# An audio tower on one core: means of the weights taken off by VectorE, a new order in the first group, and the last experts fetched in quarters and halves

## The chip, the core and the metric

The kernel runs on one core of a Trainium2 chip. The metric is the device time of the whole kernel in microseconds. Before the change it is 1425.66 us, the median of three runs (1423.68 to 1425.87). A core has five engines that run side by side: TensorE (in the profile PE for its products and PEld for its weight loads), VectorE (DVE), ScalarE (ACT), GpSimd (POOL) and SyncE (SP), which here only issues transfers. Products land in PSUM, from where VectorE or ScalarE take them to SBUF. The kernel's own schedule decides the order of the instructions of each engine; each engine works its list off in that order and waits for others by semaphores.

## What is computed

```python
h = DCT of frames of 512 samples          # 64 sequences x 157 frames x 512
n = layernorm(h)
key, query = tanh(n @ Wk + bk) * pi, tanh(n @ Wq + bq) * pi     # 4 sets x 8 planes
V = n @ Wv + bv
# per set and plane: cumulative sums of exp(i key) * V over the frames, read with exp(-i query),
# summed with softmax(set_weights); the same with fixed position phases
gate = sigmoid(n @ Wg + bg)
total = gate * total + (1 - gate) * pos_contrib
h = h + n + (total / norm) @ Wo + bo
x = layernorm(h)
# one expert of 16 per sequence, chosen by softmax(mean(x) @ Wg2 + bg2):
h = h + score * (x @ We[chosen] + be[chosen])
```

All is float32. The 64 sequences are handled in 16 groups of four. The DCT is folded into Wv, Wk, Wq and Wg, so that these weights act on the frames directly; the layernorm's mean is taken off by lowering each transformed weight by the part that the mean would carry.

## The kernel before

A group's 640 frames (four sequences of 160 slots) lie in `xT` as four chunks of 128 rows, in two halves of 320 columns. Tiles of 128 columns are numbered 0 to 3 and TAIL. PSUM is used as four buffers (`psum()`) of two banks each, handed out in turn; a new one waits for the readers of the one that had its place.

```python
def fold_once(g, m, engine=nc.gpsimd):           # first folding of the frames for the DCT
    ft = half(S[g]["xT"], m)
    add(even, ft[:, :2], ft[:, 2:])              # VectorE
    engine.tensor_tensor(ft[:, :2], ft[:, :2], ft[:, 2:], ALU.subtract)

def fold_twice(g, m):
    add(ft[:, 2], even[:, 0], even[:, 1])
    sub(ft[:, 3], even[:, 0], even[:, 1])
    for n in range(2):                           # a rotation in two lifting steps
        nc.vector.scalar_tensor_tensor(to, by, lift[:, n:n+1], to, ALU.mult, ALU.add)

def through_dct(raw, k, to, start=True, stop=True):      # a fourth of a weight through the DCT
    for i, (table, r) in enumerate(PARTS[k]):            # six products for the four fourths
        nc.tensor.matmul(to, tables[:, table], raw[:, r], ...)

def add_up(raw, n, tag, engine=nc.vector):       # sum of a weight's four fourths, in two adds

def less_mean(total, k, to):                     # the mean's share, on top of the same PSUM bank
    nc.tensor.matmul(to, tables[:, 6 + k], total, start=False, stop=True)

def centre(raw, total):                          # Wg instead: mean off ahead of the tables
    nc.tensor.matmul(ps, mean, total, start=True, stop=True)
    sub(raw, raw, ps.unsqueeze(1).to_broadcast([P, C, D]))

def embed(g, n): ...               # DCT of a tile: 8 small products into one PSUM buffer
def embed_statistics(g, n): ...    # ScalarE copy, VectorE sums and bn_stats, GpSimd rstd
def embed_res(g, n): ...           # ScalarE: residual from PSUM, which frees the buffer
def value(g, n): ...               # tile @ wv, by_tokens: four products over chunks 0..3
def keep_value(g, n): ...          # VectorE: PSUM * rstd + bv
def spread(g, n): ...              # TensorE: rstd to all rows (a transpose)
def scale(g, n): ...               # VectorE: xT tile * rstd, for keys, queries and gate
def project(g): ...                # keys and queries, ScalarE tanh to u
def phasors(g): ...                # ScalarE: eight sines of u into kf and qf
def gate_part(g, o): ...           # 128 gate columns, ScalarE tanh with bias to gT
def read(g, c): ...                # attention's reading, VectorE times and plus into gT
def weight_sums(w, t): ...         # four VectorE subtractions of 128x512, for later groups
```

The first group:

```python
warm(12)
made = [psum(), psum()]
of = [ps[:, b, :] for ps in made for b in range(2)]
for k in range(2):
    through_dct(raw_v, k, of[k], stop=False)
total = add_up(raw_v, D, "x2T")
for k in range(2, C):
    through_dct(raw_v, k, of[k], stop=False)
total_kq = add_up(raw_kq, 2 * F, "sum2")
fold_once(0, 0, nc.vector)
fold_twice(0, 0)
for k in range(C):
    less_mean(total, k, of[k])
    if k % 2:
        nc.scalar.copy(wv[:, k - 1 : k + 1], made[k // 2])
embed(0, 0)
embed(0, 1)
for k in range(C):
    through_dct(raw_kq, k, ps[:, k], stop=False)
    less_mean(total_kq, k, ps[:, k])
...
value(0, 0)
fold_once(0, 1, nc.vector); fold_twice(0, 1)
value(0, 1)
embed(0, 2); embed(0, 3)
keep(0)                              # keep_value, spread and scale of a tile together
...                                  # values 2, 3, TAIL in the same manner; Wg's sum on GpSimd
next(consts); value(0, TAIL)
fold_once(1, 0)
centre(raw_g, total)
keep(3); keep(TAIL)
...                                  # Wg through the tables, four fourths
project(0)
fold_twice(1, 0)
fold_phases(0)
...                                  # position products and constants
fold_once(1, 1)
for n in range(2):
    embed(1, n); embed_statistics(1, n)
phasors(0)
for n in range(2):
    embed_res(1, n)
# then the gate: per part of it an embedding of group 1, a spread and scale, and two of
# eight weight sums (four for wo, then four for wv); then the reads and the output products
```

The end, behind the last group (g = 15), with the experts of group 14 still to do:

```python
def fetch(g, rooms=(), parts=1, between=lambda: None):
    for k in range(parts):
        rows = ...                               # VectorE: row numbers of the chosen experts
        if k: between()
        for b in range(GB):                      # one indirect transfer per sequence
            nc.gpsimd.indirect_dma_start(out=ws[b][:, n*k : n*(k+1)], in_=of, in_offset=rows[b])

def picks(c):
    if c == 1:
        route_spread(g); pick(g)
        fetch(g, [*flat, all_v...], 2, biases)   # halves; the bias in between

expert(g - 1, ORDER[1], routes)
expert(g - 1, ORDER[2], picks)                   # picks(c) is called ahead of chunk c
...                                              # two more experts of group 14
for c in range(2):                               # chunks 0 and 1 of all five tiles,
    for n, ps in zip(order, banks):
        expert_chunk(g, n, c, ps)                # four products each, one per sequence
for n, ps in zip(order, banks):                  # then 2 and 3, tile by tile
    for c in range(2, C):
        expert_chunk(g, n, c, ps)
    expert_out(g, n, ps)
```

Of the kernel before, what the change touches and what calls it, by code (L numbers as in the profile page):

```python
# [22 lines left out]
P = 128  # L23
C = D // P
H = D // 2
GB = 4
# [20 lines left out]

ORDER = [TAIL, *range(TAIL)]


@with_exitstack
def audio_tower(ctx: ExitStack, tc: tile.TileContext, a, out):
# [30 lines left out]
    def load(name, shape, src=None):  # L83
        t = const.tile(shape, F32, name=name, tag=name)
        nc.sync.dma_start(out=t, in_=a[name] if src is None else src)
        return t
# [5 lines left out]
    def bank():  # L92
        return psum()[:, 0, :]
# [27 lines left out]

    def fold_twice(g, m):

        if g < NG:
            ft, even = half(S[g]["xT"], m), S[g].pop(("even", m))
            add(ft[:, 2], even[:, 0], even[:, 1])
            sub(ft[:, 3], even[:, 0], even[:, 1])
            for n in range(2):
                to, by = ft[:, n], ft[:, 1 - n]
                nc.vector.scalar_tensor_tensor(to, by, lift[:, n : n + 1], to, ALU.mult, ALU.add)  # L130


    def load_raw(name, n, parts=(slice(None),)):
        t = p1.tile([P, C, n], F32, tag="we", name=name, bufs=GB)
        for of in parts:
            nc.sync.dma_start(out=t[:, of], in_=a[name][:, of])
        return t

    tables = p1.tile([P, 6 + C, P], F32, tag="we", name="tables", bufs=GB)
    nc.sync.dma_start(out=tables[:, :6], in_=a["tables"])  # L140
    raw_v = load_raw("wv", D, (slice(1, C, 2), slice(0, C, 2)))
    load_half(0, 0)
    dct_e = load("dct_e", [P, 2, P])
    trig_o = load("trig_o", [P, 2, P + 1])
    lift = load("lift", [P, 2])
    nc.sync.dma_start(out=tables[:, 6:], in_=a["table_sums"].partition_broadcast(P))
    raw_kq = load_raw("wkq", 2 * F)
# [18 lines left out]
    revexp = load("revexp", [P, GB, E])  # L166
    rowbase = load("rowbase", [P, 3])

# [20 lines left out]

    def through_dct(raw, k, to, start=True, stop=True):  # L190

        for i, (table, r) in enumerate(PARTS[k]):
            nc.tensor.matmul(
                to, tables[:, table], raw[:, r], start=start and i == 0, stop=stop and i == len(PARTS[k]) - 1
            )

# [6 lines left out]

    def less_mean(total, k, to):

        nc.tensor.matmul(to, tables[:, 6 + k], total, start=False, stop=True)

    def centre(raw, total):
        ps = bank()
        nc.tensor.matmul(ps, mean, total, start=True, stop=True)
        sub(raw, raw, ps.unsqueeze(1).to_broadcast([P, C, D]))

# [13 lines left out]

    def by_tokens(ps, x, n, w):  # L230

        for c in range(C):
            nc.tensor.matmul(ps, tile_of(x[:, c], n), w[:, c, :], start=(c == 0), stop=(c == C - 1))  # L233
        return ps
# [165 lines left out]
    def value(g, n):  # L400
        s = S[g]
        s["vps", n] = by_tokens(psum()[:, 0, :], s["xT"], n, wv)

# [123 lines left out]

    def phasors(g):
        u = S[g].pop("u")
        for n, to in ((0, kf), (1, qf)):  # L530
            for k in range(2):
                rows = slice(2 * F * k + F * n, 2 * F * k + F * (n + 1))
                to_k = to.rearrange("p s b t -> p (s b t)")[:, HN * k : HN * (k + 1)]
                nc.scalar.activation(to_k[F : 2 * F], u[rows, 0], AF.Sin, scale=PI)
                nc.scalar.activation(to_k[:F], u[rows, 1], AF.Sin, bias=quarter[rows], scale=-PI)
# [181 lines left out]

    def fetch(g, rooms=(), parts=1, between=lambda: None):
        s = S[g]
        ws = [  # L720
            rooms[b] if b < len(rooms) else p1.tile([P, C * D], F32, tag="we", name="we", bufs=GB) for b in range(GB)
        ]
        n = C * D // parts
        of = a["we"].rearrange("r (k n) -> (r k) n", k=parts)
        for k in range(parts):
            rows = t("rows", [P, GB], I32)
            base = rowbase[:, parts + k - 1 : parts + k]
            nc.vector.tensor_scalar(rows, s["rev"], float(-P * parts), base, ALU.mult, ALU.add)
            if k:
                between()  # L730
            for b in range(GB):
                nc.gpsimd.indirect_dma_start(  # L732
                    out=ws[b][:, n * k : n * (k + 1)],
                    out_offset=None,
                    in_=of,
                    in_offset=bass.IndirectOffsetOnAxis(ap=rows[:, b : b + 1], axis=0),
                )
        s["ws"] = [w.rearrange("p (c o) -> p c o", c=C) for w in ws]
# [71 lines left out]
    def first_values():  # L810

        consts = constants()

        def keep(n):
            keep_value(0, n)
            spread(0, n)
            scale(0, n)

        warm(12)
        made = [psum(), psum()]  # L820
        of = [ps[:, b, :] for ps in made for b in range(2)]
        for k in range(2):
            through_dct(raw_v, k, of[k], stop=False)
        total = add_up(raw_v, D, "x2T")
        for k in range(2, C):
            through_dct(raw_v, k, of[k], stop=False)
        total_kq = add_up(raw_kq, 2 * F, "sum2")
        fold_once(0, 0, nc.vector)
        fold_twice(0, 0)
        for k in range(C):  # L830
            less_mean(total, k, of[k])
            if k % 2:
                nc.scalar.copy(wv[:, k - 1 : k + 1], made[k // 2])
        embed(0, 0)
        embed(0, 1)
        ps = bank()[:, : C * 2 * F].rearrange("p (c n) -> p c n", c=C)
        for k in range(C):
            through_dct(raw_kq, k, ps[:, k], stop=False)
            less_mean(total_kq, k, ps[:, k])
        embed_statistics(0, 0)  # L840
        nc.scalar.copy(wkq, ps)
        embed_statistics(0, 1)
        embed_res(0, 0)
        embed_res(0, 1)
        value(0, 0)
        fold_once(0, 1, nc.vector)
        fold_twice(0, 1)
        value(0, 1)
        embed(0, 2)
        embed(0, 3)  # L850
        keep(0)
        embed_statistics(0, 2)
        embed_statistics(0, 3)
        embed_res(0, 2)
        embed_res(0, 3)
        value(0, 2)
        keep(1)
        total = add_up(raw_g, D, "x2T", nc.gpsimd)
        embed(0, TAIL)
        embed_statistics(0, TAIL)  # L860
        embed_res(0, TAIL)
        value(0, 3)
        keep(2)
        next(consts)
        value(0, TAIL)
        fold_once(1, 0)
        centre(raw_g, total)
        keep(3)
        keep(TAIL)
        for k in range(C):  # L870
            if k % 2 == 0:
                ps = psum()
            through_dct(raw_g, k, ps[:, k % 2])
            if k % 2:
                nc.scalar.copy(wg[:, k - 1 : k + 1], ps)
        project(0)
        fold_twice(1, 0)
        fold_phases(0)
        next(consts)
        next(consts)  # L880
        next(consts)
        fold_once(1, 1)
        for n in range(2):
            embed(1, n)
            embed_statistics(1, n)
        phasors(0)
        for n in range(2):
            embed_res(1, n)
        weigh()

    def first_gate():

        made = chain(weight_sums(wo, t_o), weight_sums(wv, t_v))
        for n in range(C):
            gate_part(0, n)
            if n == 0:
                fold_twice(1, 1)
            m = n + 2
            if m < NM:
                embed(1, m)  # L900
                embed_statistics(1, m)
            if n == 1:
                scores(0)
            spread(1, n)
            scale(1, n)
            if m < NM:
                embed_res(1, m)
            add_bo(0, n)
            next(made)
            next(made)  # L910
        spread(1, TAIL)
        scale(1, TAIL)
        add_bo(0, TAIL)
        load_half(2, 0)
        load_half(2, 1)
# [167 lines left out]
    def picks(c):  # L1083
        if c == 1:
            route_spread(g)
            pick(g)
            fetch(g, [*flat, all_v.rearrange("p i c o -> p (i c o)")], 2, biases)

# [23 lines left out]
def _constants():  # L1112
# [15 lines left out]
    def trig(half, n, turn):  # L1128
# [12 lines left out]

    sums = [x.sum(axis=0) for x in tables]
    table_sums = np.concatenate([sums[0] + sums[1], sums[2] + sums[3], sums[4], sums[5]]) / -D
    return {
# [9 lines left out]
        "revexp": f(np.tile(E - np.arange(E), (P, GB, 1))),  # L1154
        "rowbase": f(np.stack([n * (np.arange(P) + P * E) + k for n, k in ((1, 0), (2, 0), (2, 1))], axis=1)),
    }
# [57 lines left out]
```

## Time and profile before

| | before |
|---|---|
| time | 1425.66 us (1423.68 to 1425.87) |
| span of the profiled run | 1421.9 us |
| TensorE busy | 1405.3 us, 99% |
| VectorE busy | 997.3 us, 70% |
| GpSimd busy | 607.1 us, 43% |
| ScalarE busy | 402.0 us, 28% |

Line numbers such as L233 are those of the kernel before, and a line can be that of a helper used in many places: L233 is the product of `by_tokens`, L362 that of the later groups' `product`, L601 that of `read`, L778 that of `expert_chunk`. A product in float32 shows as two passes, so `x8` in a list of TensorE's work are four calls. In brackets stands the time for which the engine was idle before, and what ended it. In a table by stretches of time the columns are the stretch, its length, the busy time and instructions of PE, PEld, DVE, ACT and POOL, the granted TensorE clock (1.00 is full), the transfers' share and GB/s.

### The profile page before, as it was taken

What the parts mean: (1) busy time and instruction counts of PE and PEld (TensorE: products, weight loads), DVE (VectorE), ACT (ScalarE), POOL (GpSimd) and SP (SyncE); (2) the same over time, 40 slices, a digit from 0 to 9 for tenths busy, and PEclk for the clock granted to TensorE, in tenths of its full rate; (3) what the DMA queues carried; (4) which work ended last, traced back from release to release, by engine and by line L of the source; (5) the groups of instructions that cost most, each with busy time, mean ns of one, the idle gap of its engine ahead of it and who ended that gap; (6) DMA issues with size and microseconds to landing.
All of it is one profiled execution on the core that took longest, in us unless ns stands there. A gap on an engine that the chain in (4) does not pass through costs nothing.

```text
span 1421.9 us, 26962 instructions
## 1 busy us (share of the span) xinstructions
PE 1405.3 (99%) x10646; PEld 929.2 (65%) x10646; DVE 997.3 (70%) x2090; ACT 402.0 (28%) x690; POOL 607.1 (43%) x849
## 2 busy tenths in 40 slices
PE   9899999999999999999999999999999999999998
PEld 5477576675757667575675757657586675766762
DVE  5677776777767676677777767677676777767573
ACT  2414242141422314232142422314223142421410
POOL 2354533535444255533535445255442545345322
PEclk9999999999999999999999999999999999999999
DMA  6013204032140322204132040322303232030305
GB/s 219 1 39 125 75 1 177 24 126 75 39 148 16 130 71 109 88 5 167 34 126 75 10 176 16 127 75 76 118 9 134 68 126 74 1 143 22 126 8 192
DMA packets 47485, 119.74 MB, mean 84 GB/s; under 512 B 9264, under 2 KB 26176, under 8 KB 39424
## 3 DMA queue, kind: packets, MB, share of 16 engines
q0 software_dynamic: 11072, 71.31, 13.0%
q1 hardware_dynamic: 35788, 46.06, 11.0%
q8 instruction: 85, 1.39, 0.4%
q10 hardware_dynamic: 500, 0.64, 0.2%
q14 instruction: 40, 0.33, 0.1%
HBM read 97.41 MB, written 20.58 MB: 83 GB/s over the span
## 4 chain that ended last, share of the span: by engine, by line
PE 91%; DVE 3%; POOL 3%; DMA 1%; issue 1%; ACT 0%; SPq 0%; DVEq 0%; POOLq 0%
PE mm L362 26%; PE mm L567 16%; PE mm L778 16%; PE mm L601 9%; PE mm L233 8%; PE mm L674 3%; PE mm L514 2%; PE mm L248 2%; PE mm L250 2%; PE mm L684 1%; POOL rstd L225 1%; PE mm L586 1%; PE mm L548 1%; PE mm L288 1%; DVE st L220 1%
## 5 line engine op out<-in xcount | busy, mean ns | idle before, releaser
L224 POOL TENSOR_SCALAR rstd<-mv 128x1 f32<-128x1 f32 x160 | 53.5, 334 | 536.1 <-DVE mv L222 529.7
L778 PE MATMUL mm<-we,x2T 128*32 128x512 f32 x2400 | 273.2, 595 | 0.5 <-DVE res_t L789 0.5
L778 PEld LDWEIGHTS mm<-we,x2T 128*32 128x32 f32 x2400 | 70.4, 109 | 149.1 <-issue 141.9
L97 DVE TENSOR_TENSOR gT<-mm,gT 128x128 f32<-128x128 f32 (+1 forms) x135 | 87.0, 672 | 88.5 <-PE mm L567 87.0
L609 DVE TENSOR_TENSOR gT<-mm,gT 128x320 f32<-128x320 f32 x256 | 116.9, 487 | 19.1 <-PE mm L601 14.7
L601 PE MATMUL mm<-att,v 32*128 32x192 f32 (+2 forms) x2048 | 127.8, 371 | 0.9 <-ACT res_t L277 0.5
L601 PEld LDWEIGHTS mm<-att,v 32*128 32x128 f32 x2048 | 105.5, 185 | 11.7 <-PE mm L601 2.9
L732 POOL DMA_INDIRECT we<-in_we,rows x60 | 64.3, 1072 | 105.1 <-issue 98.1
L97 DVE TENSOR_TENSOR v<-mm,v 128x512 f32<-128x512 f32 x105 | 70.9, 687 | 52.5 <-PE mm L362 52.5
L577 ACT ACTIVATE gT<-gT,hbg 128x320 f32<-128x320 f32 x120 | 59.6, 554 | 169.0 <-DVE gT L97 169.0
L225 POOL TENSOR_TENSOR rstd<-rstd,power 128x1 f32<-128x1 f32 x160 | 98.6, 616 | 13.4
L97 DVE TENSOR_TENSOR res<-mm,res 128x512 f32<-128x512 f32 x96 | 64.3, 684 | 56.5 <-POOL res L616 41.8
L277 ACT ACTIVATE res<-mm,shift,rstd 128x512 f32<-128x512 f32 x64 | 49.8, 778 | 158.7 <-POOL rstd L263 110.6
L661 ACT ACTIVATE x<-res,shift,rstd 128x512 f32<-128x512 f32 x64 | 52.1, 814 | 139.0 <-DVE res L97 121.9
L362 PE MATMUL mm<-t_o,sum 128*128 128x256 f32 x384 | 88.1, 379 | 0.0
L362 PE MATMUL mm<-t_v,sum 128*128 128x256 f32 x360 | 86.7, 384 | 0.0
L282 POOL TENSOR_TENSOR res<-res,bo 128x512 f32<-128x512 f32 x64 | 86.3, 1377 | 0.2 <-issue 0.2
L789 DVE SCALAR_TENSOR_TENSOR res<-mm,gate,res 128x512 f32<-128x512 f32 x64 | 48.0, 750 | 50.4 <-PE mm L288 36.4
L362 PEld LDWEIGHTS mm<-t_o,sum 128*128 128x128 f32 x384 | 71.9, 190 | 11.0
L616 POOL TENSOR_TENSOR res<-res,u 128x512 f32<-128x512 f32 x48 | 59.6, 1270 | 44.9 <-DVE u L97 44.9
L233 PE MATMUL mm<-wv,xT 128*128 128x512 f32 x160 | 72.0, 594 | 1.1 <-DVE xT L294 0.8
L119 POOL TENSOR_TENSOR xT<-xT 128x640 f32<-128x640 f32 x30 | 46.5, 1550 | 59.7 <-DVE even L97 40.7
(194 smaller groups left out, 2787.8 us busy)
## 6 DMA issues: line engine op xcount, KB each, us to landing
xT<-in_frames SPq DMA_DIRECT2D x32, 640.0 KB, 4.5
out<-res SPq DMA_DIRECT2D x248, 64.0 KB, 1.7
out<-res_t SPq DMA_DIRECT2D x62, 32.0 KB, 1.6
out<-res_t SPq DMA_DIRECT2D x62, 26.0 KB
wv<-in_wv SPq DMA_DIRECT2D x2, 512.0 KB, 5.7
wg<-in_wg SPq DMA_DIRECT2D x1, 1024.0 KB
wo<-in_wo SPq DMA_DIRECT2D x1, 1024.0 KB
we<-in_we,rows POOLq DMA_INDIRECT x60, 8.1
```

The costliest lines, as they stand in the source:

```text
L97: add = lambda *x: nc.vector.tensor_tensor(*x, ALU.add)
L225: nc.gpsimd.tensor_tensor(rstd, rstd, power, ALU.pow)
L233: nc.tensor.matmul(ps, tile_of(x[:, c], n), w[:, c, :], start=(c == 0), stop=(c == C - 1))
L282: nc.gpsimd.tensor_tensor(r, r, bo, ALU.add)
L362: nc.tensor.matmul(ps[:, b, :], lhs[:, c, P * b : P * (b + 1)], w[:, c, :], start=(c == 0), stop=(c == 1))
L567: nc.tensor.matmul(ps[:, o, :HN], w[:, c, o * P : (o + 1) * P], rhs[:, c], start=(c == 0), stop=(c == 1))
L577: nc.scalar.activation(to, to, AF.Tanh, bias=hbg[:, c : c + 1], scale=0.5)
L601: nc.tensor.matmul(to, s["v", n][q, c * P : (c + 1) * P], by, start=(n == 0), stop=(n == TAIL))
L609: nc.vector.tensor_tensor(th, r[:, :, n], th, op)
L616: more = lambda to, x: nc.gpsimd.tensor_tensor(to, to, x, ALU.add)
L732: nc.gpsimd.indirect_dma_start(out=ws[b][:, n * k : n * (k + 1)], out_offset=None, in_=of, in_offset=bass.IndirectOffsetOnAxis(ap=rows[:, ...
L778: nc.tensor.matmul(ps[Q * i : Q * (i + 1), :], s["x2T"][:, c, i, Q * n : Q * (n + 1)], s["ws"][i][:, c, :], start=(c == 0), stop=(c == C - 1),
```

## The change

It has three aims: to have TensorE do less for the weights' means, to order the first group so that TensorE waits less for the other engines, and to let the last expert products begin when a quarter of each expert's matrix is there.

The means: `through_dct` makes each fourth alone; one product with the table of means gives the mean of Wv, ScalarE copies it to SBUF, and VectorE forms `wmean * table_sums[k] + PSUM` straight into `wv`. Wk and Wq are centred ahead of their tables, as Wg is. The table of sums shrinks from 128 columns a fourth to one.

```diff
-        nc.tensor.matmul(to, tables[:, 6 + k], total, start=False, stop=True)
+        nc.tensor.matmul(ps, mean, total, start=True, stop=True)
...
-        warm(12)
-        made = [psum(), psum()]
+        warm(11)
+        side, made = psum(), [psum(), psum()][::-1]
...
+        def less_mean(k):
+            nc.vector.scalar_tensor_tensor(wv[:, k], wmean, table_sums[:, k : k + 1], of[k], ALU.mult, ALU.add)
         for k in range(2):
-            through_dct(raw_v, k, of[k], stop=False)
+            through_dct(raw_v, k, of[k])
         total = add_up(raw_v, D, "x2T")
-        for k in range(2, C):
-            through_dct(raw_v, k, of[k], stop=False)
-        total_kq = add_up(raw_kq, 2 * F, "sum2")
+        through_dct(raw_v, 2, of[2])
+        means(total, side[:, 0, :])
+        nc.scalar.copy(wmean, side[:, 0, :])
+        through_dct(raw_v, 3, of[3])
         fold_once(0, 0, nc.vector)
-        fold_twice(0, 0)
-        for k in range(C):
-            less_mean(total, k, of[k])
-            if k % 2:
-                nc.scalar.copy(wv[:, k - 1 : k + 1], made[k // 2])
+        fold_sums(0, 0)
+        total = add_up(raw_kq, 2 * F, "sum2")
+        means(total, mean_kq)
+        less_mean(2)
+        centre(raw_kq, mean_kq, 2 * F)
+        less_mean(3)
+        rotate(0, 0)
+        for k in range(C):
+            through_dct(raw_kq, k, new_kq[:, k])
+        nc.scalar.copy(wkq, new_kq)
         embed(0, 0)
         embed(0, 1)
+        less_mean(0)
+        less_mean(1)
+        value(0, 0)                      # by_tokens takes the chunks in the order 2, 3, 0, 1
+        fold_once(0, 1)                  # second half on GpSimd, not VectorE
```

The first loads are four transfers (tables 0 to 3, odd fourths of Wv, tables 4 and 5, even fourths) in place of three. The rest of the first group, as the changed kernel has it:

```python
embed_statistics(0, 0); embed_statistics(0, 1); embed_res(0, 0); embed_res(0, 1)
fold_twice(0, 1)
value(0, 1); embed(0, 2); embed(0, 3)
keep_value(0, 0); keep_value(0, 1)
...                                              # statistics and residuals of tiles 2 and 3
value(0, 2)
next(consts)
deviations(0)                                    # spread and scale
total = add_up(raw_g, D, "x2T", nc.gpsimd)
embed(0, TAIL); keep_value(0, 2); ...
value(0, 3)
means(total, ps); deviations(1); centre(raw_g, ps, D)
keep_value(0, 3); value(0, TAIL); deviations(2); keep_value(0, TAIL)
for k in range(2): through_dct(raw_g, k, made[0][:, k])
nc.scalar.copy(wg[:, :2], made[0])
deviations(3); deviations(TAIL)
for k in range(2): through_dct(raw_g, 2 + k, made[1][:, k])
fold_once(1, 0); next(sums); next(sums)          # weight sums of wv are made here
fold_twice(1, 0)
project(0)
nc.scalar.copy(wg[:, 2:], made[1])
fold_phases(0); next(consts); phasors(0, (0,))   # the keys' four sines
next(consts); next(consts)
embed(1, 0); embed_statistics(1, 0)
phasors(0, (1,))                                 # the queries' four
embed_res(1, 0); weigh(); fold_once(1, 1)
next(sums); next(sums)
# first_gate:
gate_part(0, 0); fold_twice(1, 1); embedded(1); deviations(0)   # embedded: embed, statistics, res
gate_part(0, 1); scores(0); embedded(2); deviations(1); weights()   # two weight sums of wo
gate_part(0, 2); embedded(3); embedded(TAIL); deviations(2)
gate_part(0, 3); deviations(3); deviations(TAIL); weights()
# (add_bo of a tile stands behind each deviations, as before)
```

The end:

```diff
+PIECES = [(1, 0), (4, 0), (4, 1), (2, 1)]
...
-        for k in range(parts):
-            rows = t("rows", [P, GB], I32)
+        for parts, k in pieces:          # all row numbers first
+            rows = p2.tile([P, GB], I32, tag="rows", name="rows", bufs=3)
...
-            if k:
+            if i == 1:
                 between()
...
     def picks(c):
-        if c == 1:
+        if c == 0:
...
-            fetch(g, [*flat, all_v.rearrange("p i c o -> p (i c o)")], 2, biases)
+            fetch(g, [*flat, all_v.rearrange("p i c o -> p (i c o)")], PIECES[1:], biases)
```

So the four sequences' first quarters come first, then the bias, the second quarters, and the second halves.

## The prediction

> **What bounds the kernel now.** I read the busy table first: PE 1405.3 us of a 1421.9 us span. TensorE is nearly never idle, so the change can only take TensorE work away or close TensorE's gaps. The chain of waits in order of time shows where it can do so.
>
> ```profile
> 87.60 6.11 PE mm L601 x92
> 93.71 1.92 PE mm L362 x8
> ...
> 181.50 3.43 PE mm L233 x8
> 184.93 10.36 PE mm L362 x48
> ...
> 267.33 3.43 PE mm L233 x8
> 270.77 10.36 PE mm L362 x48
> ```
>
> Columns: start, length, what. The reader is to see the period: 267.33 - 181.50 = 85.83 us a group, TensorE without a gap. The diff leaves the helpers of groups 1 to 14 as they were, so only the time up to 93.71 us (first output product of group 0) and the end behind the last group can move. The timeline of TensorE in group 0:
>
> ```profile
> 12.33 3.60 PE L209 MATMUL mm<-total,tables 128*128 128x512 f32 x8
> 20.00 7.09 PE L233 MATMUL mm<-wv,xT 128*128 128x512 f32 x16
> 29.75 3.70 PE L233 MATMUL mm<-wv,xT 128*128 128x512 f32 x8 [0.78 <-DVE xT L294]
> 45.62 0.30 PE L288 MATMUL mm<-ident,rstd 128*128 128x128 f32 x1 [2.36 <-DVE wg L96]
> 46.19 5.42 PE L196 MATMUL mm<-wg,tables 128*128 128x512 f32 x12 [0.28 <-DVE v L411]
> 63.85 0.84 PE L248 MATMUL mm<-dct_e,xT 128*128 128x128 f32 x4 [2.63 <-issue]
> 84.34 2.09 PE L601 MATMUL mm<-att,v 32*128 32x320 f32 x26 [0.52 <-ACT res_t L277]
> ```
>
> L209 is the mean taken off by eight passes. The brackets are idle time and its cause. Behind the gap at 63.85 stands a PSUM buffer: that embedding wants one which `embed_res(1, 0)` on ScalarE frees, and this is queued behind eight sines. By stretch of time the gap costs twice, as the clock (the third number from the right) shows:
>
> ```profile
> 62.00:63.00 1.00, 0.00 (x0) 0.00 (x0) 0.20 (x1) 0.96 (x3) 0.81 (x3) 1.00 0.00 0
> 66.00:67.00 1.00, 1.00 (x4) 0.72 (x3) 0.00 (x0) 0.99 (x2) 0.00 (x0) 0.50 0.00 0
> ```
>
> At the end, the timeline of GpSimd and of the weight loads, then the two pieces of the chain:
>
> ```profile
> 1388.57 1.07 POOL L732 DMA_INDIRECT wv<-in_we,rows  x1 [8.73 <-DVE logit L744]
> 1392.44 0.94 POOL L732 DMA_INDIRECT t_v<-in_we,rows  x1 [0.30 <-issue]
> 1398.68 0.94 POOL L732 DMA_INDIRECT t_v<-in_we,rows  x1 [0.30 <-issue]
> 1400.28 0.11 PEld L778 LDWEIGHTS mm<-t_v,x2T_last 128*32 128x32 f32 x1 [1.35 <-DMA t_v<-in_we,rows]
> ```
>
> ```profile
> 1392.44 7.80 DMA t_v<-in_we,rows
> 1400.28 17.37 PE mm L778 x154
> ```
>
> TensorE could have begun the last expert products at 1395.56 (its first matmul on `wv`). The fourth half matrix lands at 1400.28: 4.7 us lost. After it come 40 passes at 0.43 us without a gap.
>
> [...] after a gap of 2.63 us, 0.50 was granted near 65.4 to 68.5. [...] the trace has 0.74 for such a SCALAR_TENSOR_TENSOR (L411), which I use. [...] 4.8 us at least, 7.9 median, from issue to landing of 512 KB in this stretch.
>
> **Part 1, Wv's and Wk/Wq's means.** Gone from TensorE: eight passes of L209 on Wv (3.43 us on the chain) and eight small ones on Wk/Wq. Added: one product with the mean table on each (0.87 us as L213, about 0.2). Added on VectorE: four SCALAR_TENSOR_TENSOR of 128x512 from PSUM, 4 x 0.74 = 3.0 us, and a subtraction of 128x256, some 0.4. The weights load in four transfers with 128 KB less ahead of the first product: at about 310 GB/s, 0.4 us earlier, so it starts near 6.6.
>
> VectorE is now the chain here. `wv` is whole at 8.84 as before; add_up 1.23 + 0.69 to 10.76; first folds 2 x 0.82 to 12.45; sums 2 x 0.48 to 13.4; Wk/Wq sum 0.5 to 13.9; then less_mean 0.74, centre 0.4, less_mean 0.74, rotate 1.13, less_mean 2 x 0.74, to 18.4. The first value product needs the last of these and starts at 18.4 against 20.0. So 3.2 us of TensorE work saved gives 1.6 us.
>
> **Part 2, order in the rest of the values.** spread and scale come later, so the token products no longer wait for VectorE's 0.69 (L294) between them. With 6.9 us for values 0 and 1, 1.8 for two embeddings and 3.45 a value, the third starts at 27.1 (29.75 before), the fourth at 31.8 (35.04). The fifth waits for the buffer of the last embedding, near 37.3. Wg's mean product follows GpSimd's add_up, near 35.6, and VectorE takes it off by 39.9 (2.29 us, L96). Now TensorE has the fifth value under that (37.3 to 40.75), where it stood idle for 2.36 us. Wg's table products run 41.0 to 46.6 with two transposes between, and the projection starts at 46.6 against 51.53: 4.9 us.
>
> **Part 3, into the gates.** Projection 2.3 us to 48.9; then ScalarE's tanh (0.53) and the second copy of Wg (1.01), which also frees the PSUM buffer for the position products, to 50.6; these 1.1 and one embedding 0.9; the first gate part starts at 52.6 (56.74). Only one embedding of group 1 precedes it, and `embed_res` stands after the second set of sines, near 57.8, when the gate part (4.3 us, to 56.95) has just ended. The second gate part starts at 58.2 instead of 66.06: 7.9 us, since the 2.63 us gap and the half clock (about 3.1 us x 0.5 = 1.6) both go. Then a new wait: the next embedding needs `embed_res(1, 1)`, behind VectorE's fold_twice(1, 1), sums and statistics, near 64.9, while TensorE is through the scores at 63.65: 1.25 us. The third gate part starts at 66.1 (73.83), the fourth at 72.5 (79.14), the reads at 77.8 (84.34).
>
> The reads then follow VectorE: the last deviations and t_o sums hold it to 79.9, and four reads at 1.93 us each (L609) let TensorE finish the fourth near 85.5 to 86.5. Before, the four t_v subtractions (0.69, 0.71, 0.90 and 1.76 us) stood before the last scaling and held the reads back to 93.64. By hand the first output product comes 7.1 to 8.1 us earlier.
>
> **Part 4, the last experts.** The spread moves one chunk earlier (0.86 us), but VectorE is in order: it takes `logit` at 1386.27, straight after add_bias, in both kernels. So the first fetch stays at 1388.57. Issues are 1.245 us apart (1388.57 + 3 steps of which the first is 1.38) whatever the size: a 1 MB fetch also shows 0.94 us. Quarters double the issues of the first half, from 9 to 13 in all. With 3.8 to 4.5 us from issue to landing for 256 KB (4.8 for 512 KB less 0.6 of data at 420 GB/s, or some queueing): the fourth quarter is issued at 1392.4 and lands near 1396.6; chunk 0 of five tiles takes 4.3 us, to 1400.9; the eighth quarter is issued at 1398.7 and lands at 1402.7: 1.8 us lost; chunk 1 to 1407.0; the fourth half is issued at 1403.7 and lands near 1408.4: 1.4 us lost. The remaining 8.6 us end at 1417.0 against 1417.65. The 3.7 us won at the start are given back twice: about 0.5 us are left, between -1 and +1.5.
>
> **Sum.** 7.6 us in group 0 and 0.5 at the end, 8.1 by hand. A hand schedule leaves out small waits, and VectorE is slower beside GpSimd's work (the same t_v subtraction takes 0.69 to 1.76 us, L96), so I take off 0.8: 7.3 us. 1425.66 - 7.3 is 1418.4.
>
> **Rivals.** (1) VectorE's longer chain at the start eats the saving: between 12.6 and 15.1 TensorE is idle for about 2 us in two pieces, and if the clock falls as it did at 65 us, 3 us of value products run at half speed, another 1.6 us. Against it: the gaps are shorter than 2.63 us. Then about 1420. (2) TensorE's gap in group 0 merely moves from 63 to about 64 us, into the wait for `embed_res(1, 1)`; if GpSimd's fold is slow it grows to 3 us and brings the half clock back: 3 us of the gain gone, about 1421. (3) The quarters overlap better than I think and the end gains 3 us: about 1415. (4) The issue time of thirteen fetches makes the end longer by 1 us: about 1420. The first two would have to come together to leave no gain at all, as nothing in groups 1 to 14 changes.
>
> **Range and chances.** The four spread the time from 1415 to 1422; with a noise of some 1 us (1423.68 to 1425.87 before) the range is 1414.8 to 1421.8. Two per cent is 28.5 us, more than all of TensorE's gaps together (1421.9 - 1405.3 = 16.6) plus the work removed, so faster by over 2% gets 0.01, slower 0.01, the rest 0.98.
>
> **What would show it.** Right: the first value product near 18.4 us, the projection near 46.6, no gap over 2 us between the first and second gate part, the first output product (L362's line) near 86, a group still 85.8 us; at the end two waits for the fourth tile in place of one. Wrong: a granted clock of 0.5 before 30 us, a gap over 2.5 us near 64, or reads that end later than 88; and for the end, a last expert product that ends before 1408 or after 1411 on the new scale (7 us earlier).

## The result, and the profile after

| | before | changed | ratio, 95% interval |
|---|---|---|---|
| time, first series | 1425.76 us | 1430.1 us (1429.49 to 1433.14) | 1.0037 [1.002, 1.0055] |
| time, second series | 1424.93 us | 1428.94 us (1427.87 to 1432.35) | 1.0029 [1.0018, 1.0039] |
| span of the profiled run | 1421.9 us | 1431.4 us | |
| TensorE busy | 1405.3 us | 1409.2 us | |

The kernel became 4 us slower; the prediction was 1418.4 us, 7.3 us faster. Line numbers are those of the changed kernel from here on: L240 is the product of `by_tokens`, L369 that of `product`, L610 that of `read`, L792 that of `expert_chunk`, L295 the transpose of `spread`, L557 the gate part. The chain of waits of the changed kernel, in order of time (start, length, what):

```profile
97.65 1.92 PE mm L369 x8
...
1403.84 0.82 issue
1404.65 0.60 PE mm L792
...
1410.30 16.53 PE mm L792 x146
```

The first line answers to 93.71 of before: the first output product of group 0 comes 3.9 us later, not 7 to 8 earlier. The middle is as predicted: from that product to the first fetch of the last experts it is 1294.8 us (97.65 to 1392.43) against 1294.9 (93.71 to 1388.57). At the end, the last pieces in which TensorE runs through are about the same length (16.53 and 17.37), but what stands ahead of them is new: single passes of 0.6 us with pieces called "issue" between, for which the profile finds no releaser. TensorE's timeline in group 0:

```profile
20.17 7.34 PE L240 MATMUL mm<-wv,xT 128*128 128x512 f32 x16
62.81 0.32 PE L295 MATMUL mm<-ident,rstd 128*128 128x128 f32 x1 [2.18 <-POOL rstd L232]
64.17 6.26 PE L557 MATMUL mm<-xT,wg 128*128 128x320 f32 x16 [1.03 <-ACT res L284]
85.41 0.32 PE L295 MATMUL mm<-ident,rstd 128*128 128x128 f32 x1 [2.14 <-POOL rstd L232]
86.77 3.58 PE L610 MATMUL mm<-att,v 32*128 32x320 f32 x32 [1.04 <-ACT res_t L284]
```

The old gap of 2.63 us at 63.85 is gone, and two gaps of more than 3 us in two pieces each stand in its place, one ahead of the second gate part and one ahead of the reads. By stretch of time, a granted clock of 0.50 follows both (third number from the right):

```profile
66.00:67.00 1.00, 1.00 (x3) 0.68 (x2) 0.95 (x3) 0.38 (x2) 0.00 (x0) 0.50 0.00 0
88.00:89.00 1.00, 1.00 (x16) 0.84 (x12) 1.00 (x1) 0.00 (x0) 1.00 (x2) 0.50 0.65 233
```

So the second gate part takes 6.26 us (5.77 in the kernel before, 4.47 at the granted 1.00 of the first part), and the reads begin slowly. At the end, GpSimd's timeline (first and fourth quarter, then the last half):

```profile
1392.43 1.09 POOL L746 DMA_INDIRECT wv<-in_we,rows  x1 [9.34 <-DVE logit L758]
1396.33 0.95 POOL L746 DMA_INDIRECT t_v<-in_we,rows  x1 [0.30 <-issue]
1407.61 0.94 POOL L746 DMA_INDIRECT t_v<-in_we,rows  x1 [0.30 <-issue]
```

Thirteen issues at 1.25 us, as predicted. But TensorE comes to full speed (four passes at once every 0.43 us) only at 1411.04, 18.6 us after the first issue; before, it was 11.7 (1388.57 to 1400.28).

### The profile page after: what moved, and what is told of

It is laid out like the page before. It is cut to its first block, busy times and chain, and to the rows that moved or that the text cites. A ratio compares the mean times of both kernels' runs of the same rounds, so it can differ in the third digit from the quotient of the medians.

```text
span 1431.4 us, 26950 instructions
## 1 busy us (share of the span) xinstructions
PE 1409.2 (98%) x10632; PEld 929.8 (65%) x10632; DVE 999.8 (70%) x2095; ACT 400.3 (28%) x689; POOL 612.1 (43%) x854
## 4 chain that ended last, share of the span: by engine, by line
PE 90%; DVE 4%; POOL 4%; issue 1%; ACT 1%; DMA 0%; SPq 0%; POOLq 0%; DVEq 0%; ACTq 0%
PE mm L369 26%; PE mm L792 17%; PE mm L576 16%; PE mm L610 9%; PE mm L240 8%; PE mm L683 3%; PE mm L521 2%; PE mm L255 2%; PE mm L257 2%; POOL rstd L232 1%; PE mm L693 1%; DVE st L227 1%; PE mm L595 1%; POOL rstd L231 1%; PE mm L295 1%
## 5 line engine op out<-in xcount | busy, mean ns | idle before, releaser
L792 PE MATMUL mm<-we,x2T 128*32 128x512 f32 x2400 | 273.8, 595 | 0.6 <-DVE res_t L803 0.5
L792 PEld LDWEIGHTS mm<-we,x2T 128*32 128x32 f32 x2400 | 70.5, 109 | 150.1 <-issue 144.1
L610 PE MATMUL mm<-att,v 32*128 32x192 f32 (+2 forms) x2048 | 129.6, 377 | 1.0 <-ACT res_t L284 1.0
L610 PEld LDWEIGHTS mm<-att,v 32*128 32x128 f32 x2048 | 106.6, 188 | 12.3 <-PE mm L610 2.9
L369 PE MATMUL mm<-t_o,sum 128*128 128x256 f32 x384 | 88.1, 379 | 0.0
L369 PE MATMUL mm<-t_v,sum 128*128 128x256 f32 x360 | 86.7, 384 | 0.0
L369 PEld LDWEIGHTS mm<-t_o,sum 128*128 128x128 f32 x384 | 71.9, 190 | 11.0
L240 PE MATMUL mm<-wv,xT 128*128 128x512 f32 x160 | 72.3, 596 | 1.4 <-ACT res_t L284 1.1
```

The source lines that it names most:

```text
L369: nc.tensor.matmul(ps[:, b, :], lhs[:, c, P * b : P * (b + 1)], w[:, c, :], start=(c == 0), stop=(c == 1))
L610: nc.tensor.matmul(to, s["v", n][q, c * P : (c + 1) * P], by, start=(n == 0), stop=(n == TAIL))
L792: nc.tensor.matmul(ps[Q * i : Q * (i + 1), :], s["x2T"][:, c, i, Q * n : Q * (n + 1)], s["ws"][i][:, c, :], start=(c == 0), stop=(c == C - 1),
```

## Experiments

All times against runs of the kernel before on the same chip:

| run | what | us | ratio [95%] |
|---|---|---|---|
| after_again | the changed kernel | 1428.94 | 1.0029 [1.0018, 1.0039] |
| tail_only | before + the new fetch | 1430.73 | 1.0043 [1.0029, 1.0056] |
| group_only | the new first group, old fetch | 1425.38 | 1.0000 [0.9992, 1.0009] |
| loads_back | group_only + old first loads | 1425.44 | 1.0003 [0.9994, 1.0012] |
| idle_issues | before + 4 idle issues behind the weights | 1430.34 | 1.0042 [1.0026, 1.0057] |
| half_quarters | tail_only, half first, quarters last | 1430.32 | 1.0039 [1.0025, 1.0052] |
| late_issues | before + 4 idle issues some 6 us later | 1425.30 | 0.9997 [0.9988, 1.0005] |
| whole | before, 1 MB pieces, 5 issues | 1429.68 | 1.0032 [1.002, 1.0044] |
| order_only | group_only, one order in the gate | 1422.82 | 0.9984 [0.9976, 0.9993] |
| room_only | group_only, two subtractions later | 1423.43 | 0.9986 [0.9978, 0.9995] |
| order_room | both | 1419.41 | 0.9965 [0.9952, 0.9979] |
| order_room_gate | both + a gate part earlier | 1420.50 | 0.9969 [0.9957, 0.998] |

### Which half of the change loses

My first theory was that the first group loses, as its first output product comes 3.9 us later in the profile; the rival was the fetch of the last experts. The edits: tail_only takes `fetch`, `PIECES` and `c == 0` of the change into the kernel before. The other two go the other way:

```
# group_only: the changed kernel with
PIECES = [(1, 0), (2, 0), (2, 1)]        # was (1,0), (4,0), (4,1), (2,1)
if c == 1:                               # was c == 0
# loads_back: group_only with
nc.sync.dma_start(out=tables, in_=a["tables"])       # one transfer, then wv's two
```

> The changed kernel a second time, for a second profile and a firmer time. If its profile is typical, group 0 again ends near 97.6 us (3.9 us later than before) and TensorE crawls again at about 0.7 us a pass between the first quarter's landing and the last half's, with some 36 to 39 us from the first fetch to the end (33.3 before). If the crawl was an accident of that one execution, the stretch from the first fetch to the end is 33 to 35 us. Time 1429.5 to 1431.

> The kernel before with nothing but the new fetches: quarters, quarters, halves, asked for one chunk earlier. Theory G (the loss of 4.3 us lies in the first group, the tail is neutral): within 0.7 us of before. Theory T (thirteen issues and the smaller transfers make the end late): slower by 2 us or more. The prediction's own sum had 0.5 us faster.

> The changed kernel with before's fetches in halves at the end. Theory G: slower than before by 3.5 to 4.5 us, as all of the loss is in group 0 and nothing comes back. Theory T: slower by less than 2.5 us. The first output product stays near 97.6 us in either.

> As group_only, with the first loads again as before: all six tables in one transfer, then the odd and the even fourths of Wv. In the changed kernel's trace the first product started at 7.90 us instead of 7.00 and VectorE had Wv at 9.60 instead of 8.84. If the four transfers are the cause, these return to 7.0 and 8.8, and the first output product comes about 0.8 us earlier unless a later wait swallows it (then the time equals group_only's).

My theory fell. The fetch alone loses 5.8 us (1430.73 against 1424.93); the first group alone neither loses nor gains. after_again shows the crawl a second time: 39.7 us from the first fetch to the end, where the kernel before took 33.3. The two profiles had misled me: the first output product moves from run to run, and the profile of the changed kernel is of the slowest of its four runs (1433.14 us). In after_again that product starts at 96.10. The first group of before has it at 93.64 in its own profile and at 94.97, 95.17, 95.16, 95.22 and 93.29 in those of tail_only, half_quarters, idle_issues, late_issues and whole, which leave that group as it was; group_only has 95.45. The split first loads bring nothing that can be measured.

### What loses in the fetch: size, or number of issues

In tail_only the fourth quarter's last packet ends some 7.5 us after the first issue (1389.95; an estimate, as packets are counted by their bytes in the order of their starts). The prediction had 8.0, so the data come about as predicted. Yet TensorE works single passes until 1408.56, 3.4 us behind the start of the last issue. Two runs part the number of issues from their size:

```
# idle_issues: before, behind the last half
+ for k in range(4):                     # 16 rows of 64 bytes, read by nobody
+     nc.gpsimd.indirect_dma_start(out=scrap, in_=..., in_offset=...expi[:16])
# half_quarters: tail_only with
PIECES = [(1, 0), (2, 0), (4, 2), (4, 3)]
```

> The kernel before with four idle transfers issued by GpSimd behind the last half of the last experts' weights: each gathers 16 rows of 64 bytes into a tile that nobody reads. Nothing else differs, so the weights are issued and land as before. Issue theory (formed on the traces of the quarters: in each of six profiles TensorE works the last group's first chunk one pass at a time until 1.6 to 3.5 us after the start of GpSimd's last issue, and only then at full speed): four more issues of 1.25 us each put that off by 5.0 us, so the kernel takes about 1430 us (1428.5 to 1431). Size theory (the quarters lose because pieces of 256 KB move fewer bytes per issue, so that data come late): no data come later here, so 1425 us (1424 to 1426.5).

> The run tail_only with the pieces in another order of sizes: first half, third quarter, fourth quarter, so still 13 issues, but the first piece is the half of before. Issue theory: 13 issues end as late as in tail_only, so TensorE comes to full speed 5 us later than before: about 1430.5 us (1429 to 1432). Size theory: the first chunks come as before (512 KB per issue) and only the last two quarters trickle, which are wanted last: 1425 to 1427.5 us.

Both lose 5.4 us: the issue theory holds, the size theory falls. TensorE and GpSimd in the timelines of idle_issues (`wv`, `wg`, `spare` and `t_v` are the tiles in which the expert matrices of the four sequences lie):

```profile
1400.84 0.62 PE L778 MATMUL mm<-t_v,x2T_last 128*32 128x512 f32 x1 [0.31 <-DMA t_v<-in_we,rows]
1404.23 0.60 PE L778 MATMUL mm<-spare,x2T_last 128*32 128x512 f32 x1 [0.83 <-issue]
1408.47 0.61 PE L778 MATMUL mm<-wg,x2T_last 128*32 128x512 f32 x1
```

```profile
1400.15 0.94 POOL L732 DMA_INDIRECT t_v<-in_we,rows  x1 [0.30 <-issue]
1404.86 0.84 POOL L1090 DMA_INDIRECT scrap<-in_be,expi  x1 [0.30 <-issue]
```

At 1400.84 the fourth half has landed and TensorE passes on at once, as in the kernel before. It has all it needs for the chunk, and still goes a pass at a time until 3.6 us behind the start of the last idle issue. An idle issue of 1 KB takes 0.84 us and 0.30 between, nearly what one of 512 KB takes. Set side by side over the profiles:

| profile | first issue | last issue of the row | full speed | behind the last |
|---|---|---|---|---|
| before (9 issues) | 1388.57 | 1398.68 | 1400.28 | 1.6 |
| group_only (9) | 1390.22 | 1400.30 | 1403.16 | 2.9 |
| loads_back (9) | 1390.53 | 1400.64 | 1403.48 | 2.8 |
| changed kernel (13) | 1392.43 | 1407.61 | 1411.04 | 3.4 |
| after_again (13) | 1390.94 | 1406.11 | 1409.57 | 3.5 |
| tail_only (13) | 1389.95 | 1405.12 | 1408.56 | 3.4 |
| idle_issues (13) | 1390.05 | 1404.86 | 1408.47 | 3.6 |
| half_quarters (13) | 1389.98 | 1405.09 | 1408.45 | 3.4 |

With 13 issues full speed comes 18.4 to 18.6 us after the first issue; with 9 in the row, in all eight profiles of this record, it is 11.7 to 13.0. The difference of 5.5 to 6.9 us is four issues of 1.25 and 0.5 to 1.9 more. That is the loss (5.4 to 5.8 us in the times). The slow passes were there with nine issues too, only shorter and partly hidden in the waits for the data.

### Does an issue slow TensorE at any time, and do fewer help

```
# late_issues: before, behind the last add_bias: the four idle issues,
#              with indices that VectorE writes only then
# whole: before with the last experts in pieces (1, 0), the biases' fetch last
```

> The kernel before with the same four idle transfers as in idle_issues, but behind the biases of the last experts, so that GpSimd issues them at about 1405 to 1410 us, when TensorE has been at full speed for some 5 us on the last experts. If an issue by GpSimd slows TensorE at any moment in which it works on the last experts, its matmuls fall to one pass per 0.7 us again for some 5 us: 1429 to 1431 us. If what is slow is only the start of the last experts (the passes up to the end of a row of issues that was running when TensorE came to them), nothing changes: 1424.5 to 1426 us.

> The kernel before with the last experts' weights in whole tiles of 1 MB: five issues instead of nine, the last of them (the biases) 5 us earlier. Issue theory: no slow passes are left behind the issues, but the fourth tile lands only behind 4 MB instead of 2 MB, at the 235 to 420 GB/s of the trace of before 15 to 19 us after the first issue instead of 11.7; TensorE stands in waits for a DMA, not in unexplained ones: 1428 to 1432 us. Rival (the slow passes come from the amount of bytes on the way and not from the issues): slow passes without a releaser are seen as before, up to the landing of the fourth tile.

late_issues costs nothing. The timelines of GpSimd and of TensorE (the passes on one of the four tiles):

```profile
1407.39 0.85 POOL L1109 DMA_INDIRECT scrap<-in_be,late  x1 [6.33 <-DVE late L1106]
```

```profile
1407.54 0.59 PE L778 MATMUL mm<-wg,x2T_last 128*32 128x512 f32 x1
1407.97 0.59 PE L778 MATMUL mm<-wg,x2T_last 128*32 128x512 f32 x1
1408.40 0.59 PE L778 MATMUL mm<-wg,x2T_last 128*32 128x512 f32 x1
```

GpSimd issues from 1407.39 to 1411.7, and TensorE keeps its 0.43 us from pass to pass. So these four issues did not slow a TensorE that was already at full speed on these tiles; what was slow is the start, while the row of issues still runs (in idle_issues its last four fetch nothing for these tiles). In whole the row ends early (last issue 1393.25), and the slow passes are gone; TensorE waits for data instead, with the releaser named:

```profile
1400.31 1.92 PE L786 MATMUL mm<-spare,x2T_last 128*32 128x512 f32 x2 [1.74 <-DMA spare<-in_we,rows]
1403.26 1.06 PE L786 MATMUL mm<-t_v,x2T_last 128*32 128x512 f32 x1 [1.03 <-DMA t_v<-in_we,rows]
```

The fourth tile comes 15.1 us after the first issue, and behind these waits the granted clock is 0.50 (1404 to 1405; 1.06 us a pass instead of 0.59). Too few issues lose by data, too many by issues; of the numbers that ran, 5, 9 and 13, nine is the best.

### Where the first group's gain went

In group_only TensorE is 3.4 us ahead of before's profile at the first gate part (53.30 against 56.74) and not ahead of it at the reads (84.77 against 84.34; 84.00 to 85.92 in the other profiles that leave the group as it was). Two waits took it. The first, in the timeline of the changed kernel (all engines):

```profile
59.82 2.29 POOL L231 TENSOR_SCALAR rstd<-mv 128x1 f32<-128x1 f32 x1 [5.34 <-DVE mv L229]
60.01 0.81 DVE L98 TENSOR_TENSOR even<-xT 128x640 f32<-128x640 f32 x1
60.75 0.68 DVE L97 TENSOR_TENSOR t_v<-wv,t_v 128x512 f32<-128x512 f32 x1
61.35 0.68 DVE L97 TENSOR_TENSOR t_v<-wv 128x512 f32<-128x512 f32 x1
```

An addition on 128 numbers, 0.21 to 0.32 us at its nine other places in group 0, takes 2.29 us on GpSimd beside three VectorE operations of 0.81 + 0.68 + 0.68 = 2.17 us, and the transpose, the residual and the second gate part wait for it. It ends at 62.11, just behind the last of them (62.03); what holds it up is not shown beyond that. The change had put the two `t_v` subtractions there. The second wait, on ScalarE of the changed kernel:

```profile
81.79 0.78 ACT L284 ACTIVATE res<-mm,shift,rstd 128x512 f32<-128x512 f32 x1 [3.58 <-POOL rstd L270]
82.47 0.26 ACT L265 COPY sines<-mm 128x129 f32<-128x129 f32 x1
85.94 0.78 ACT L284 ACTIVATE res_t<-mm,shift,rstd 128x512 f32<-128x512 f32 x1 [3.21 <-POOL rstd L270]
```

ScalarE took these in the order of its list: the residual of part 3 waits 3.58 us for GpSimd, and only then, at 82.47, comes a copy of 0.26 us with which the tail's statistics begin. So two chains of VectorE, GpSimd and ScalarE run one after the other, and the reads need the second one's end. The edits, each on group_only:

```
# order_only                          # room_only
- embedded(3)                         - next(sums); next(sums)   # behind weigh(), fold_once(1, 1)
- embedded(TAIL)                      + next(sums); next(sums)   # behind gate_part(0, 2)
+ embed(1, 3); embed(1, TAIL)
+ embed_statistics(1, 3); embed_statistics(1, TAIL)
+ embed_res(1, 3); embed_res(1, TAIL)
# order_room: both. order_room_gate: both, and gate_part(0, 1) straight behind gate_part(0, 0)
```

> group_only (the changed first group, last experts in halves) with one change of order in the gate of the first group: the embeddings of part 3 and of the tail are both made, then both statistics, then both residuals, so that ScalarE copies the tail's sines ahead of the residual of part 3, which waits for GpSimd. Order theory (in-order ScalarE holds up the tail's statistics, and so the reads): the 2.1 us wait for rstd and the 0.9 us wait for res_t ahead of the reads shrink, the reads start 1.5 to 3 us earlier and at full clock, first output product 92 to 93.5 instead of 95.4: 1421.5 to 1424 us. Rival (the stretch is bound elsewhere, by VectorE's chain or by the matmuls themselves): first output product stays within 0.7 us, 1424.5 to 1426 us.

> group_only with the last two differences of the value weights (two VectorE subtractions of 0.6 us) moved from the end of the phases, where GpSimd's 128x1 operation on the deviation of part 0 took 2.29 us beside them, to the gate, behind its third part. Room theory (GpSimd's small chain is held up by VectorE's run of work, and with it embed_res and the second gate part): rstd of part 0 takes 0.3 us again, the wait of 2.2 us ahead of the second gate part goes and its matmuls run at full clock, so the second part ends 2 to 4 us earlier; the first output product 92.5 to 94 if the wait ahead of the reads does not take it back: 1422 to 1425 us. Rival (gaps only move: the reads still wait for the tail's residual): second gate part earlier but reads within 0.7 us of before, 1424.5 to 1426 us.

> group_only with both edits of order_only and room_only, last experts in halves as in the kernel before. If the two losses of the first group are separate (a wait ahead of the second gate part, a wait ahead of the reads), the gains add: 2.6 + 2.0 us below group_only, about 1421 us (1419.5 to 1422). If they are one loss that only moves, no better than the better of the two: 1422.5 to 1424 us.

> order_room with the second gate part handed to TensorE straight behind the first, ahead of the embedding of part 1 and of the transpose for part 0. In the trace of room_only two waits of 1.0 us each stood ahead of the second gate part, and the part then took 6.26 us at half clock instead of 4.47. Gap theory: both waits go and the clock stays full, so the first output product comes 2 to 3.8 us earlier than in order_room: 1417.5 to 1419.5 us. Rival (the transposes and embeddings behind it now wait instead, and the later parts take the gain back): within 1 us of order_room.

Against group_only's 1425.38, order_only gains 2.6 us, room_only 2.0, both together 6.0 (5.0 by the ratios to before, 0.9965 against 1.0000). So the two losses are separate. In room_only the addition on GpSimd takes 1.08 us, beside the one VectorE operation that is left (0.81), again ending just behind it (58.41 and 58.33), and the wait is 0.97 us instead of 2.17. In order_only the tail's residual waits 0.70 us instead of 3.2. GpSimd in room_only, then ScalarE in order_only:

```profile
57.33 1.08 POOL L231 TENSOR_SCALAR rstd<-mv 128x1 f32<-128x1 f32 x1 [5.34 <-DVE mv L229]
```

```profile
81.85 0.78 ACT L284 ACTIVATE res_t<-mm,shift,rstd 128x512 f32<-128x512 f32 x1 [0.70 <-POOL rstd L270]
```

TensorE in order_room:

```profile
59.07 0.32 PE L295 MATMUL mm<-ident,rstd 128*128 128x128 f32 x1 [0.97 <-POOL rstd L232]
60.41 4.58 PE L557 MATMUL mm<-xT,wg 128*128 128x320 f32 x16 [1.02 <-ACT res L284]
79.27 2.09 PE L610 MATMUL mm<-att,v 32*128 32x320 f32 x26 [0.70 <-ACT res_t L284]
88.91 1.99 PE L369 MATMUL mm<-wo,gT 128*128 128x256 f32 x8
```

The second gate part takes 4.58 us instead of 6.26 in this profile, and the 2.14 us wait ahead of the reads is gone. The 4.58 is not the edits' doing alone: room_only has the same order up to there and the same two waits (0.97 and 1.03), yet took 6.26 us for the part, against its expectation, as the changed kernel did at a granted clock of 0.50; over the whole run the mean granted clock is 0.996 in room_only's profile and 1.000 in order_room's. The first output product comes 4.7 us before that of before's profile. order_room_gate does close the waits ahead of the second part (both parts run as one piece of 8.78 us), but waits of 1.25 and 1.49 us then stand ahead of the third part, which takes 6.27 us instead of 4.57: the gap theory fell, the gap moved.

order_room, the change with its last experts in halves again and two edits of order, beats both kernels.

## Why the prediction was wrong

Point by point, with the starts of TensorE's pieces in us:

| stage | before | predicted | group_only | changed | order_room |
|---|---|---|---|---|---|
| first value product | 20.00 | 18.4 | 18.51 | 20.17 | 17.95 |
| projection | 51.53 | 46.6 | 47.91 | 49.89 | 47.34 |
| first gate part | 56.74 | 52.6 | 53.30 | 55.27 | 52.73 |
| second gate part | 66.06 | 58.2 | 62.19 | 64.17 | 60.41 |
| third gate part | 73.83 | 66.1 | 70.51 | 72.49 | 67.57 |
| reads | 84.34 | 77.8 | 84.77 | 86.77 | 79.27 |
| first output product | 93.64 | 85.5 to 86.5 | 95.45 | 97.58 | 88.91 |

**Right: the means' work.** Part 1 holds to 0.1 us in group_only, Part 2 to 1.3 us at the projection. So close a fit is partly luck: in the eight profiles with the new first group the first value product starts between 17.95 and 20.17. In the changed kernel's own profile the stage is 2 us later: its first weights came late (first product at 7.90, in the other profiles of this group 6.2 to 6.7), and the granted clock was 0.50 from 17.4 to 20.8. That is rival 1. It showed, between 15.5 and 20.8, in five of these eight profiles, in halves of embeddings that took up to 1.17 us (0.61 to 0.66 in the other three), and from the first product to the first value product those took 12.3 to 13.4 us instead of 11.3 to 12.0. I had held against it that the gaps are short; they were, 0.53 and 0.51 us in the changed kernel, and the clock fell all the same.

**Wrong, first step: the gates of Part 3, with "a new wait" of 1.25 us behind the second part, and the reads at 77.8.** I put `embed_res(1, 0)` near 57.8, counting nothing for GpSimd's small chain ahead of it. It ran at 63.34 in the changed kernel and at 61.36 in group_only, as the subtractions which I had counted as gone from the gate held GpSimd up where the change put them. Counted from the start of the first gate part it was to come after 5.2 us; it came after 8.1 in group_only and after 6.9 in order_room. So the subtractions made 1.2 us of the delay, and the rest of GpSimd's chain 1.7. And I let the tail's statistics follow their embedding at once, as if ScalarE's order did not matter. The two waits, with the granted 0.50 behind them, are rival 2's kind of loss at two places. It had given them 3 us; the edits that shorten them bring 5 to 6 us, which shows that they took at least that much of the 7.6. Part of the rest lies in the reads: from their start to the first output product they take 9.6 us in order_room (9.3 before), where I had counted 7.7 to 8.7; why is not shown. The prediction also says that rivals 1 and 2 together would leave no gain: as I priced them they come to 1.6 + 3 = 4.6 us, so that sum was wrong.

**Wrong, second step: Part 4, "The 3.7 us won at the start are given back twice: about 0.5 us are left".** The issue spacing was right, and the quarters landed when I said. What failed is the unspoken rule that a matmul starts when its data are there. TensorE came to full speed only 3.4 us behind the last of thirteen issues, idle ones counted like full ones. Rival 4 had the cause, "The issue time of thirteen fetches", but gave it 1 us where the runs give 5.4 to 5.8.

**The sum.** Predicted -7.6 and -0.5 with 0.8 taken off; measured 0 for the group and +5.8 for the end. The changed kernel lost about 4 us. That the two do not quite add is not shown: the interval of tail_only, [1.0029, 1.0056], overlaps that of the changed kernel, [1.0018, 1.0039].

**Open.** Why TensorE crawls there is not shown. It is not missing data (idle_issues). It is not the bytes or the number of gathers on the way: the idle issues carry 4 KB, and in the kernel before TensorE is at full speed from 1400.28 while packets of the second halves come until 1407.7. And it is not GpSimd issuing as such: group 14's last experts run at full speed beside the first five issues, and late_issues beside four more. The recorded passes are mostly spaced by 0.7 us or multiples of it, at a granted clock of 1.00. VectorE, too, comes late to group 14's last expert: in tail_only it takes it at 1408.68, as TensorE comes to full speed, though its last matmul is recorded at 1397.18.

## What to carry to other kernels

Count the issues of a row of gathers as work that stands in series with their first reader (1.25 us each here): a smaller first piece comes sooner but makes the row longer, and here the reader was at full speed only when the row had ended. When TensorE work is taken away, look next at the smallest operations on the chain that the freed time now waits for (here an addition of 0.2 us that took 2.29, and a copy of 0.26 us behind a wait of 3.58): which instructions run beside them, and what stands ahead of them in the list of their engine. The profile of one run lay 2 us off another in one stage here (17.95 and 20.17 for the first value product), so run the parts of a change apart before blaming the stage where two profiles differ.

## What the runs showed of the hardware

- A gather issued by GpSimd holds it for 1.25 us (0.94 and 0.30 between) at 256 KB (tail_only) and 512 KB (before) alike, and for 1.15 us with 16 rows of 64 bytes. In whole it is 1.24 us for 1 MB.
- TensorE started slowly on freshly gathered tiles while the row of gathers was still being issued, until 1.6 to 3.6 us behind the start of the last issue; once at full speed it was not slowed by four further issues (late_issues).
- A GpSimd addition on 128x1 took 0.21 us with no VectorE operation beside it (changed kernel, 38.51), 1.08 beside one addition of 0.81 us (room_only, 57.33) and 2.29 beside three additions and subtractions of 0.81, 0.68 and 0.68 us (changed kernel, 59.82). It took 0.22 at 68.36 in the changed kernel, beside a scaling of 0.65 us (L301), so not every VectorE operation beside it cost time.
- A granted clock of 0.50 came in stretches of 3.4 us or twice that: 65.3 to 68.7 in before's profile; 17.4 to 20.8, 65.2 to 68.6 and 85.6 to 92.5 in the changed kernel's. It fell after short gaps too: in the changed kernel at 17.4 us, with two gaps of 0.53 and 0.51 us in the 5 us ahead of it. Gaps of 1.03 and 0.51 us at the same place did not bring it in room_only, where the halves of the embeddings behind them took 0.61 to 0.66 us (0.81 to 1.07 in the changed kernel), so what sets it off is not settled by these runs.
